# Layer 0's input held as 128 + 64 channels: the group norm, the channel norm and two projections in a new layout

## The chip, the cores and the metric

The kernel runs on one core of one Trainium2 chip. The metric is the device time of one execution in microseconds (us), the smaller the better. The profile is one execution recorded by the hardware profiler; its engines are PE (TensorE matrix multiplies), PEld (the loading of their weights), DVE (VectorE), ACT (ScalarE), POOL (GpSimd) and SP (SyncE, which issues DMAs). Everything is float32.

## The reference, cut to what matters

The input `x` is 16 images of 192 channels by 32 x 32 pixels (1024 pixels each). Four layers follow one another; each adds its result to `x`. Only layer 0 is touched here:

```python
def _gn(v, G=32, eps=1e-5):            # group norm: 32 groups of 6 channels
    g = v.reshape(B_, G, C_ // G, H_, W_)
    m = mean(g, axis=(2, 3, 4)); s = var(g, axis=(2, 3, 4))
    return ((g - m) / sqrt(s + eps)).reshape(v.shape)

# layer 0, on xg = _gn(x); seq is xg as (image, pixel, channel)
h = layernorm(seq) * ln_w + ln_b       # over the 192 channels of a pixel
x_in, z = split(h @ w_up + b_up)       # 192 -> 2 x 384
x_act = silu(causal_conv4(x_in) + conv_b)
q, k, v = x_act @ w_q, x_act @ w_k, x_in
hs = mlstm_scan(q, k, v, gates(q, k, v))          # 12 heads of 32, over 1024 pixels
x1 = seq + ((norm(hs) * mh_w + mh_b + skip * x_act) * silu(z)) @ w_down + b_down
x2 = silu(seq @ w_lin + b_lin)
y = conv3x3(x1 + x2, conv2_w) + conv2_b           # then batch norm over all images
```

Layers 1 to 3 follow for all images (a convolutional attention, a selective scan in four directions, a shift mixer), and take most of the time.

## The kernel before, in words

`layer0` works on one image at a time. Image 0 is written out; images 1 to 15 are 15 turns of a hardware loop (`tc.For_i`, line 753) whose body is `both()` and `image(b, conv3(b - 1))`. Between two turns all engines wait for one another. Within a turn the 3 x 3 convolution of the image before (`conv3`, line 393, tiles `pc`, `ypad`, `w_c`, `w_c2p`) is mixed into this image's work: a part by the tile scheduler, a part at fixed places by `fill(n)` in a stretch with a hand-made order (`tc.manual_schedule`). Outside that stretch the scheduler sets the order of each engine's instructions; each engine then runs its list strictly in that order, and waits where an input is missing.

The 192 channels of `x` lie as two blocks of 96 on 96 partitions (`P6`), each with all 1024 pixels. An image starts like this:

- `group_norm`: four `bn_stats` of 512 pixels (line 90), two `bn_aggr` (line 91), and one matmul with `blk6` (96 x 96, 1/6 inside a group) that gives the means of the groups (line 93, result 96 x 2). Four small DVE steps later a second matmul with `blk6` gives the variances (line 101); then square root on ACT (line 103), reciprocal, and two DVE instructions that write the normalised `xn` (line 109).
- `xnext`, the buffer of the input, is filled for the next image as soon as `xn` is written (line 408, one DMA on SP's queue).
- `channel_norm`: per half of the pixels two matmuls with a 96 x 96 matrix of 1/192 (`on`, line 39 is the helper `matmuls`) give the mean over channels in all rows; DVE subtracts it (line 124), ACT squares (line 126), two matmuls per half sum the squares, ACT takes logarithm and exponential for 1/sqrt (lines 130, 131), and DVE multiplies (line 133), which gives `h`.
- The up projection: for six groups `m` of 128 outputs and two halves, two matmuls of contraction 96 (line 39, `ps<-h,w_up`). For `m` < 3 DVE adds the bias and writes `x_in` (line 427), on which DVE does the causal convolution (lines 437, 441) and ACT the silu (line 445); for `m` >= 3 ACT writes `sz` (line 432).
- Gates: 24 matmuls on column tiles of 32 (line 457) into one PSUM tile, which ACT copies as `raw` (line 464); `spread` matmuls (line 468), scans on DVE, and meanwhile the q and k projections.

In the hand-ordered stretch follow the scores and the chunks of the recurrence (lines 586 to 689). At the end of the image `w_lin` (contraction 96 x 2, on `xn`) and `w_down` (128 x 3) are multiplied for 128 channels of either half and for the last 64 channels of both halves side by side (line 733), and ACT and DVE combine them with the input into `ypad` (lines 737 to 741). For that last step the input is wanted in the layout of the output, and four DMAs on SP's queue make a copy `xr` of `xn` in it (lines 718 to 722).

A matmul of float32 runs on the chip as two passes, each with its own loading of weights; the profile counts each pass.

Of the kernel before, what the change touches and what calls it, by code (L numbers as in the profile page):

```python
# [11 lines left out]
F32 = mybir.dt.float32  # L12
BF16 = mybir.dt.bfloat16
AF = mybir.ActivationFunctionType
ALU = mybir.AluOpType
# [4 lines left out]
C, H, W = 192, 32, 32  # L20
L = H * W
HL = L // 2
P6 = 96
INNER, NH, DH = 384, 12, 32
# [7 lines left out]
def half(hf):  # L32
    return slice(hf * HL, (hf + 1) * HL)


def matmuls(nc, out, pairs):
    n = len(pairs)
    for i, (l, r) in enumerate(pairs):
        nc.tensor.matmul(out, lhsT=l, rhs=r, start=(i == 0), stop=(i == n - 1))


class Ctx:


    def __init__(self, tc, cpool, I):
        self.tc, self.nc, self.I = tc, tc.nc, I
        self.ordered = False
        self.table = None
        nc = self.nc
        self.ident = cpool.tile([128, 128], F32, name="ident")  # L50
        nc.sync.dma_start(self.ident, I["c_ident"])
        self.blk6 = cpool.tile([P6, P6], F32, name="blk6")
        nc.sync.dma_start(self.blk6, I["c_blk6"])
        self.eps5 = cpool.tile([128, 1], F32, name="eps5")
        nc.vector.memset(self.eps5, 1e-5)
        self.one = cpool.tile([128, 1], F32, name="one")
        nc.vector.memset(self.one, 1.0)
        self.on192 = cpool.tile([P6, P6], F32, name="on192")
# [21 lines left out]
        return self.ident[0:k, j : j + 1].to_broadcast([k, m])  # L80


def group_norm(cx, pool, ps, src, dsts):

    nc = cx.nc
    st = pool.tile([P6, 2, 2, 6], F32, tag="gn_st", name="gn_st")
    mv = pool.tile([P6, 2, 2], F32, tag="gn_mv", name="gn_mv")
    for a in range(2):
        for hf in range(2):
            nc.vector.bn_stats(st[:, a, hf, :], src[:, a, half(hf)])  # L90
        nc.vector.bn_aggr(mv[:, a, :], st[:, a].rearrange("p h s -> p (h s)"))
    p = ps()
    nc.tensor.matmul(p[0:P6, 0:2], lhsT=cx.blk6, rhs=mv[:, :, 0], start=True, stop=True)
    mg = pool.tile([P6, 2], F32, tag="gn_mg", name="gn_mg")
    nc.vector.tensor_copy(mg, p[0:P6, 0:2])
    d = pool.tile([P6, 2], F32, tag="gn_d", name="gn_d")
    nc.vector.tensor_sub(d, mv[:, :, 0], mg)
    nc.vector.tensor_mul(d, d, d)
    nc.vector.tensor_add(d, d, mv[:, :, 1])
    p2 = ps()  # L100
    nc.tensor.matmul(p2[0:P6, 0:2], lhsT=cx.blk6, rhs=d, start=True, stop=True)
    rs = pool.tile([P6, 2], F32, tag="gn_rs", name="gn_rs")
    nc.scalar.activation(rs, p2[0:P6, 0:2], AF.Sqrt, bias=cx.eps5[0:P6])
    nc.vector.reciprocal(rs, rs)
    for a in range(2):
        s = src[:, a, :]
        if len(dsts[a].shape) == 3:
            s = s.rearrange("p (h w) -> p h w", w=W)
        nc.vector.tensor_scalar(
            dsts[a], s, mg[:, a : a + 1], rs[:, a : a + 1], op0=ALU.subtract, op1=ALU.mult  # L110
        )


def channel_norm(cx, ps, ones, src, dst, sq, rstd):

    nc = cx.nc
    cx.ln_exp()
    np_ = src.shape[0]
    n = src.shape[1]
    for hf in range(2):  # L120
        pm = ps()
        matmuls(nc, pm[0:np_, :], [(ones, src[:, g, half(hf)]) for g in range(n)])
        for g in range(n):
            nc.vector.tensor_sub(dst[:, g, half(hf)], src[:, g, half(hf)], pm[0:np_, :])
    for g in range(n):
        nc.scalar.activation(sq[:, g, :], dst[:, g, :], AF.Square)
    for hf in range(2):
        pv = ps()
        matmuls(nc, pv[0:np_, :], [(ones, sq[:, g, half(hf)]) for g in range(n)])
        nc.scalar.activation(rstd[:, half(hf)], pv[0:np_, :], AF.Ln, bias=cx.eps5[0:np_])  # L130
    nc.scalar.activation(rstd, rstd, AF.Exp, scale=-0.5)
    for g in range(n):
        nc.vector.tensor_mul(dst[:, g, :], dst[:, g, :], rstd)


def depthwise3(nc, out, pad, w):
# [18 lines left out]
def layer0(tc, cx, NB, ydram, sdram, w1d):  # L155
    nc, I = cx.nc, cx.I
    with ExitStack() as ctx:
# [18 lines left out]
            eng.dma_start(t, v.rearrange("(a p) -> p a", p=p))  # L176
            return t

        xnext = wp.tile([P6, 2, L], F32, name="xnext")
        nc.sync.dma_start(xnext, I["x"][0].rearrange("(a p) l -> p a l", p=P6))  # L180
        w_up = wp.tile([P6, 2, 2 * INNER], F32, name="w_up")
        nc.scalar.dma_start(w_up, I["w_up"].rearrange("(a p) o -> p a o", p=P6))
        ln_w, ln_b = vec("ln_w", P6), vec("ln_b", P6)
        b_up = vec("b_up", 128)

        pre = ctx.enter_context(ExitStack())
# [118 lines left out]
        for m in range(6):  # L305
            matmuls(
                nc, p[:, m : m + 1],
                [(w_up[:, a, m * 128 : (m + 1) * 128], ln_b[:, a : a + 1]) for a in range(2)],
            )
        nc.vector.tensor_add(b_up, b_up, p[:, 0:6])  # L310
        for a in range(2):
# [17 lines left out]


        w_down = wp.tile([128, 3, C], F32, name="w_down")
        w_lin = wp.tile([P6, 2, C], F32, name="w_lin")
        for t, nm, p in ((w_down, "w_down", 128), (w_lin, "w_lin", P6)):
            nc.sync.dma_start(t, I[nm].rearrange("(k p) o -> p k o", p=p))
        w_c2 = wp.tile([128, 9, C], F32, name="w_c2")
        nc.sync.dma_start(w_c2, I["conv2_wT"][0:128])
        w_c2p = wp.tile([128, 2, 3, C], F32, name="w_c2p")
# [65 lines left out]
                nc.scalar.dma_start(stats(slice(128, C))[:, 6 * hf : 6 * hf + 6], st[r, 2, :])  # L403

        def image(b, conv):
            xn = big.tile([P6, 2, L], F32, name="xn")
            group_norm(cx, sm, ps, xnext, [xn[:, 0, :], xn[:, 1, :]])
            nc.sync.dma_start(
                xnext,
                I["x"][bass.ds((b + 1) % NB, 1)].rearrange("o (a p) l -> p (o a) l", p=P6),  # L410
            )
            h = big.tile([P6, 2, L], F32, tag="h", name="h")
            sq = big.tile([P6, 2, L], F32, tag="kT", name="sq")
            rstd = big.tile([P6, L], F32, tag="fc", name="rstd")
            channel_norm(cx, ps, cx.on192, xn, h, sq, rstd)


            sz = big.tile([128, 3, L], F32, name="sz")
            for m in range(6):
                for hf in range(2):  # L420
                    p = ps()
                    matmuls(
                        nc, p,
                        [(w_up[:, a, m * 128 : (m + 1) * 128], h[:, a, half(hf)]) for a in range(2)],
                    )
# [288 lines left out]
                pass  # L714


            xr = big.tile([128, 3, HL], F32, tag="qT", name="xr")
            nc.sync.dma_start(xr[0:P6, 0:2, :].rearrange("p h l -> p (h l)"), xn[:, 0, :])
            nc.sync.dma_start(xr[P6:128, 0:2, :].rearrange("p h l -> p (h l)"), xn[0:32, 1, :])
            lower, upper = slice(0, 64), slice(64, 128)  # L720
            for hf, r in enumerate((lower, upper)):
                nc.sync.dma_start(xr[r, 2, :], xn[32:P6, 1, half(hf)])

            for n in range(3):
                e = n // 2
                parts = [(n, slice(0, 128), slice(0, 128))] if n < 2 else [
                    (0, slice(128, C), lower), (1, slice(128, C), upper)
                ]
                pl, pd = ps(), ps()
                for p, w_, v, k in ((pl, w_lin, xn, 2), (pd, w_down, hT, 3)):  # L730
                    for i in range(k):
                        for hf, o, r in parts:
                            nc.tensor.matmul(
                                p[r, :], lhsT=w_[:, i, o], rhs=v[:, i, half(hf)], start=(i == 0), stop=(i == k - 1)
                            )
                lin = wk2.tile([128, HL], F32, tag="lin", name="lin")
                nc.scalar.activation(lin, pl, AF.Silu, bias=b_lin[:, e : e + 1])
                nc.vector.tensor_add(lin, lin, xr[:, n, :])
                for hf, o, r in parts:
                    x = 0 if r == upper else 1  # L740
                    nc.vector.scalar_tensor_tensor(
# [1351 lines left out]
def constants():  # L2093
# [7 lines left out]
    helmert[DH - 1] = 0.0  # L2101
    return {
        "c_ident": np.eye(128, dtype=f),
        "c_blk6": ((q[:, None] // 6 == q[None, :] // 6) / 6.0).astype(f),
        "c_causal": np.where(p[:, None] <= p[None, :], 0.0, NEG).astype(f),
        "c_hmask": (p[:, None] // DH == np.arange(4 * HW1)[None, :] // HW1).astype(f),
# [66 lines left out]
```

## Time and profile before

| | |
|---|---|
| median of 3 runs | 14432.32 us (14414.68 to 14432.79) |
| the profiled execution | 14423.57 us, span of its instructions 14421.8 us |
| layer 0, from the span's start | about 3055 us of it |
| starts of the turns for images 7, 8 and 9 (first `bn_stats`, line 90) | 1346.74, 1534.80 and 1725.62 us |
| `raw` copy (line 464) of images 7 and 8 | 1391.71 and 1581.19 us |
| busy share of the span | PE 84%, DVE 82%, POOL 76%, ACT 60% |
| mean granted TensorE clock | 0.924 |

Views of the profile used below: stretches of time with each engine's busy time and the granted TensorE clock (PEclk, 1.00 is full speed); the timeline, with runs of the same instruction merged (start in us, us that they span, engine, line, operation, out<-in, rows*columns of the array, out shape, number, and in brackets idle time of the engine ahead of it with what ended it); and the answers for one line of the source (duration of one in ns: least, median, most; then first and last start in us). The ends of matmuls are modelled and pipelined, so distances between starts tell more than durations.

### The profile page before, as it was taken

To read this page: it belongs to the slowest core of one execution; us is meant where nothing else is said; L and a number is where in the kernel's file an instruction comes from. 1 tells how busy PE (TensorE), PEld (TensorE's weight loads), DVE (VectorE), ACT (ScalarE), POOL (GpSimd) and SP (SyncE) were. 2 spreads that over 40 slices of the span, in tenths; PEclk is the share of its full clock that TensorE was granted. 3 is DMA by queue.
4 is the path that set the end of the run, shared out by engine and by line. 5 is a ranking of instruction groups with operands and counts; after the bars stand their busy time and mean duration, and the time that the engine had idled before them with its cause. 6 is when DMAs were issued, how large, how long until landed. Compare 5 with 4: busy or idle time off the path is not lost. (4 is left out here: it accounts for less than half of the span.)

```text
span 14421.8 us, 185702 instructions
## 1 busy us (share of the span) xinstructions
PE 12156.5 (84%) x68912; PEld 4993.1 (35%) x68912; DVE 11832.7 (82%) x9085; ACT 8688.4 (60%) x12229; POOL 10928.7 (76%) x6319
## 2 busy tenths in 40 slices
PE   8999999987888888888888888788888888888877
PEld 4444444442233333333333333333333333333323
DVE  4444444447899999999999999999999999999996
ACT  3333333336667676767676666676676767676655
POOL 2222222216799999999999999999999999999995
PEclk9999999998999999999999999998999999999888
DMA  1000000014344444444444445444444444444432
GB/s 29 15 16 16 15 16 16 16 40 131 128 157 143 157 154 159 153 143 158 143 158 141 160 145 164 142 159 137 162 134 164 147 157 162 145 152 150 144 122 90
DMA packets 702528, 1707.95 MB, mean 118 GB/s; under 512 B 125456, under 2 KB 260065, under 8 KB 693985
## 3 DMA queue, kind: packets, MB, share of 16 engines
q1 hardware_dynamic: 688928, 1693.28, 36.0%
q8 instruction: 556, 9.11, 0.3%
q10 hardware_dynamic: 12736, 3.04, 0.1%
q14 instruction: 308, 2.52, 0.1%
HBM read 1338.12 MB, written 341.15 MB: 116 GB/s over the span
## 5 line engine op out<-in xcount | busy, mean ns | idle before, releaser
L1994 POOL TENSOR_TENSOR xs<-du,bb 128x1024 f32<-128x1024 f32 x3072 | 7196.6, 2364 | 424.9 <-DVE h L2002 418.5
L2002 DVE TENSOR_TENSOR_SCAN h<-h,xs 128x1024 f32<-128x1024 f32 x2688 | 6150.8, 2288 | 385.5 <-ACT h L1987 296.1
L1987 ACT ACTIVATE h<-dl,A 128x1024 f32<-128x1024 f32 x3072 | 3413.9, 1113 | 2420.4 <-DVE hc L2011 2268.5
L2011 DVE TENSOR_TENSOR hc<-h,cb 128x1024 f32<-128x1024 f32 x2688 | 3290.6, 1224 | 264.9 <-DVE h L2002 4.6
L817 PE MATMUL mm<-pad,dg 128*128 128x512 f32 (+1 forms) x5580 | 2667.4, 616 | 120.3 <-DMA dg<-dvd 39.9
L2044 PE MATMUL acc<-hc,sel 128*32 128x256 f32 x24576 | 2016.5, 415 | 800.5 <-DVE hc L2011 600.5
L629 POOL TENSOR_TENSOR D<-D,mask 128x256 f32<-128x256 f32 x768 | 543.6, 741 | 2101.7 <-DVE D L626 2101.7
L2044 PEld LDWEIGHTS acc<-hc,sel 128*32 128x32 f32 x24576 | 549.6, 112 | 2745.4 <-DVE hc L2011 1397.2
L817 PEld LDWEIGHTS mm<-pad,dg 128*128 128x128 f32 (+1 forms) x5580 | 958.7, 182 | 1494.0 <-issue 1285.7
L2007 POOL TENSOR_TENSOR hc<-hc,cb 128x1024 f32<-128x1024 f32 x384 | 905.7, 2359 | 205.1 <-DVE hc L2002 201.9
L817 PE MATMUL mm<-pa,wgt 128*128 128x512 f32 (+1 forms) x1408 | 781.6, 681 | 208.0 <-ACT pb L817 119.6
L2052 PE MATMUL acc<-ones,zero 128*128 128x512 f32 x1648 | 901.6, 678 | 0.0
L2002 DVE TENSOR_TENSOR_SCAN hc<-h,xs 128x1024 f32<-128x1024 f32 x384 | 875.6, 2280 | 16.7 <-ACT h L1987 12.5
L817 POOL TENSOR_TENSOR dlh<-dlh,e 128x512 f32<-128x512 f32 x384 | 489.4, 1275 | 233.5 <-ACT e L817 230.9
L817 POOL TENSOR_TENSOR c<-cx 96x768 f32<-96x768 f32 (+4 forms) x510 | 650.2, 1298 | 2.5 <-PE mm L817 2.5
L817 PE MATMUL mm<-c,xT 128*96 128x256 f32 x2048 | 575.9, 423 | 69.0 <-ACT c L817 68.2
L2031 PE MATMUL acc<-y,ident 128*128 128x512 f32 x576 | 354.2, 700 | 250.1 <-ACT y L2063 248.8
L817 POOL TENSOR_TENSOR duh<-dlh,xx 128x512 f32<-128x512 f32 x384 | 538.1, 1401 | 30.1
L393 PE MATMUL pc<-ypad,w_c 128*64 128x512 f32 (+1 forms) x1152 | 480.3, 664 | 74.3 <-PEq L753 41.5
L2063 ACT COPY y<-acc 128x512 f32<-128x512 f32 x384 | 411.4, 1071 | 150.7 <-PE acc L2044 149.9
L626 DVE SCALAR_TENSOR_TENSOR D<-D,s 128x256 f32<-128x256 f32 x768 | 271.7, 416 | 255.6 <-ACT D L622 255.6
L2052 PEld LDWEIGHTS acc<-ones,zero 128*128 128x128 f32 x1648 | 329.4, 215 | 431.8 <-issue 429.5
(334 smaller groups left out, 15907.5 us busy)
## 6 DMA issues: line engine op xcount, KB each, us to landing
dl<-dld SPq DMA_DIRECT2D x768, 512.0 KB
du<-dud SPq DMA_DIRECT2D x768, 512.0 KB
bb<-xdr SPq DMA_DIRECT2D x256, 512.0 KB
cb<-xdr SPq DMA_DIRECT2D x256, 512.0 KB
dld<-dlh SPq DMA_DIRECT2D x384, 256.0 KB
dud<-duh SPq DMA_DIRECT2D x384, 256.0 KB
dg<-dqd SPq DMA_DIRECT2D x270, 192.0 KB
dg<-dvd SPq DMA_DIRECT2D x180, 144.0 KB
```

Of the source, the lines that this page charges most:

```text
L393: nc.tensor.matmul(p[r, :], lhsT=w_, rhs=v, start=(n == 0), stop=(n == 14))
L629: nc.gpsimd.tensor_mul(d, d, mask)
L817: return f(out, *args, **kw)
L1987: self.nc.scalar.activation(self.h[u % 2], self.dl[n % 2], AF.Exp, scale=self.A[:, blk, n : n + 1])
L1994: self.nc.gpsimd.tensor_mul(self.xs[u % 3], self.du[n % 2], self.bb[blk])
L2002: self.nc.vector.tensor_tensor_scan(o, h, x, 0.0, op0=ALU.mult, op1=ALU.add)
L2007: self.nc.gpsimd.tensor_mul(h, h, self.cb[u % BLOCKS])
L2011: self.nc.vector.tensor_mul(self.hc[u % 3], self.h[u % 2], self.cb[u % BLOCKS])
L2031: nc.tensor.matmul(acc, lhsT=self.cx.ident, rhs=self.y[:, g, half(pair)], start=True, stop=False)
L2044: nc.tensor.matmul(self.acc[rows4(q), q4(s)], lhsT=self.sel, rhs=part(q), start=False, stop=(s + blk == BLOCKS),)
L2052: self.nc.tensor.matmul(self.acc, lhsT=cx.zero.to_broadcast([128, 128]), rhs=cx.ones.unsqueeze(1).to_broadcast([128, 4, 128]), start=False ...
L2063: self.nc.scalar.copy(y.rearrange("p (s w h) -> p s h w" if k % 2 == 0 else "p (s h w) -> p s w h", s=2, **turn), self.acc.rearrange("p (s ...
```

## The change

The input is held as the output's layout wants it: `xnext`, `xn`, `h`, `sq` and `rstd` become [128, 3, 512]: slots 0 and 1 hold channels 0 to 127 of either half of the pixels, slot 2 holds channels 128 to 191 of the first half on partitions 0 to 63 and of the second half on partitions 64 to 127. Weights with the channels as rows (`w_up`, `w_lin`, `ln_w`, `ln_b`) are loaded with the last 64 rows twice, once for either half of the partitions (`twice`). Where two blocks of 96 rows were contracted, now 128 rows are, and then the two halves' 64 rows one after the other, on the upper and the lower 64 rows of the array. The group sums take a new constant `mix` (2 x 2 blocks of 128 x 128) and eight matmuls with one column in place of two with two. `xr` and its four DMAs go; the input is fetched by three DMAs in place of one.

```diff
-    for a in range(2):
-        for hf in range(2):
-            nc.vector.bn_stats(st[:, a, hf, :], src[:, a, half(hf)])
-        nc.vector.bn_aggr(mv[:, a, :], st[:, a].rearrange("p h s -> p (h s)"))
-    p = ps()
-    nc.tensor.matmul(p[0:P6, 0:2], lhsT=cx.blk6, rhs=mv[:, :, 0], start=True, stop=True)
+    for n in range(3):
+        nc.vector.bn_stats(st[:, n, :], src[:, n, :])
+    nc.vector.bn_aggr(mv[:, 0, :], st[:, 0:2, :].rearrange("p h s -> p (h s)"))
+    nc.vector.bn_aggr(mv[:, 1, :], st[:, 2, :])
+    def groups(v):
+        p = ps()
+        for j in range(2):
+            matmuls(nc, p[:, j : j + 1], [(mix[:, i, j, :], v[:, i : i + 1]) for i in range(2)])
+        return p[:, 0:2]
+    p = groups(mv[:, :, 0])
...
-    p2 = ps()
-    nc.tensor.matmul(p2[0:P6, 0:2], lhsT=cx.blk6, rhs=d, start=True, stop=True)
+    p2 = groups(d)
...
+    def sums(v):                       # channel_norm: for the means and for the squares
+        p = [ps() for _ in range(2)]
+        on = cx.on192.to_broadcast([128, 128])
+        for hf in range(2):
+            nc.tensor.matmul(p[hf], lhsT=on, rhs=v[:, hf, :], start=True, stop=False)
+        for hf, r in enumerate(rows2):
+            nc.tensor.matmul(
+                p[hf], lhsT=cx.on192[r].to_broadcast([64, 128]), rhs=v[r, 2, :], start=False, stop=True
+            )
+        return p
+    p = sums(src)
+    for hf, r in enumerate(rows2):
+        nc.vector.tensor_sub(dst[:, hf, :], src[:, hf, :], p[hf])
+        nc.vector.tensor_sub(dst[r, 2, :], src[r, 2, :], p[hf][r])
+    for n in range(3):
+        nc.scalar.activation(sq[:, n, :], dst[:, n, :], AF.Square)
+    p = sums(sq)
+    for hf, r in enumerate(rows2):
+        nc.scalar.activation(rstd[:, hf, :], p[hf], AF.Ln, bias=cx.eps5)
+        nc.scalar.activation(rstd[r, 2, :], p[hf][r], AF.Ln, bias=cx.eps5[r])
     nc.scalar.activation(rstd, rstd, AF.Exp, scale=-0.5)
+    nc.vector.tensor_mul(dst, dst, rstd)
...
             for m in range(6):
-                for hf in range(2):
-                    p = ps()
-                    matmuls(nc, p,
-                        [(w_up[:, a, m * 128 : (m + 1) * 128], h[:, a, half(hf)]) for a in range(2)])
+                pair, o = [ps() for _ in range(2)], slice(m * 128, (m + 1) * 128)
+                for hf, p in enumerate(pair):
+                    nc.tensor.matmul(p, lhsT=w_up[:, 0, o], rhs=h[:, hf, :], start=True, stop=False)
+                for p, r in zip(pair, (lower, upper)):
+                    nc.tensor.matmul(p, lhsT=w_up[r, 1, o], rhs=h[r, 2, :], start=False, stop=True)
...
-            xr = big.tile([128, 3, HL], F32, tag="qT", name="xr")
-            nc.sync.dma_start(xr[0:P6, 0:2, :].rearrange("p h l -> p (h l)"), xn[:, 0, :])
-            nc.sync.dma_start(xr[P6:128, 0:2, :].rearrange("p h l -> p (h l)"), xn[0:32, 1, :])
...
+            pls = [ps() for _ in range(3)]
+            for i in range(2):
+                for n in range(4):
+                    m, hf = min(n, 2), n % 2
+                    r, o = ((lower, upper)[hf], slice(128, C)) if m == 2 else (slice(0, 128), slice(0, 128))
+                    k = (slice(0, 128), (lower, upper)[hf])[i]
+                    nc.tensor.matmul(
+                        pls[m][r, :], lhsT=w_lin[k, i, o], rhs=xn[k, 2 if i else hf, :], start=(i == 0), stop=(i == 1)
+                    )
...
-                nc.vector.tensor_add(lin, lin, xr[:, n, :])
+                nc.vector.tensor_add(lin, lin, xn[:, n, :])
```

The program that results has these differences in the order of PE's list in a loop turn. Before: two convolution matmuls, the group means (1 matmul), one convolution matmul, the group variances (1), four convolution matmuls, the channel means (4), three convolution matmuls, the sums of squares (4), four convolution matmuls, the up projection (24). After: one convolution matmul, the group means (4), one convolution matmul, the group variances (4), four convolution matmuls, the channel means (2 of 128 rows, then the pair of 64 rows), one convolution matmul, the first square sum, one convolution matmul, the second square sum, the pair, six convolution matmuls, the up projection (six times 2 and a pair). The number of convolution matmuls ahead of the up projection is 14 in both. At the end of the image the `w_lin` matmuls all stand ahead of the `w_down` ones. POOL's list is the same in both, and the lists of all engines behind layer 0 are the same but for two small memsets on DVE.

More of the change, by code (lines that the diff above doesn't have):

```diff
@@ L57, in __init__ @@
         nc.vector.memset(self.one, 1.0)
-        self.on192 = cpool.tile([P6, P6], F32, name="on192")
+        self.on192 = cpool.tile([128, 1], F32, name="on192")
         nc.vector.memset(self.on192, 1.0 / C)
@@ L80, in onehot, with group_norm @@
         return self.ident[0:k, j : j + 1].to_broadcast([k, m])
-def group_norm(cx, pool, ps, src, dsts):
+def group_norm(cx, pool, ps, src, dst, mix):
     nc = cx.nc
-    st = pool.tile([P6, 2, 2, 6], F32, tag="gn_st", name="gn_st")
-    mv = pool.tile([P6, 2, 2], F32, tag="gn_mv", name="gn_mv")
-    for a in range(2):
-        for hf in range(2):
-            nc.vector.bn_stats(st[:, a, hf, :], src[:, a, half(hf)])
-        nc.vector.bn_aggr(mv[:, a, :], st[:, a].rearrange("p h s -> p (h s)"))
-    p = ps()
[L93 to L96, printed above, removed]
+    st = pool.tile([128, 3, 6], F32, tag="gn_st", name="gn_st")
+    mv = pool.tile([128, 2, 2], F32, tag="gn_mv", name="gn_mv")
+    for n in range(3):
[8 more added lines that the diff above has]
+    p = groups(mv[:, :, 0])
+    mg = pool.tile([128, 2], F32, tag="gn_mg", name="gn_mg")
+    nc.vector.tensor_copy(mg, p)
+    d = pool.tile([128, 2], F32, tag="gn_d", name="gn_d")
     nc.vector.tensor_sub(d, mv[:, :, 0], mg)
@@ L99, in group_norm @@
     nc.vector.tensor_add(d, d, mv[:, :, 1])
-    p2 = ps()
-    nc.tensor.matmul(p2[0:P6, 0:2], lhsT=cx.blk6, rhs=d, start=True, stop=True)
-    rs = pool.tile([P6, 2], F32, tag="gn_rs", name="gn_rs")
-    nc.scalar.activation(rs, p2[0:P6, 0:2], AF.Sqrt, bias=cx.eps5[0:P6])
+    p2 = groups(d)
+    rs = pool.tile([128, 2], F32, tag="gn_rs", name="gn_rs")
+    nc.scalar.activation(rs, p2, AF.Sqrt, bias=cx.eps5)
     nc.vector.reciprocal(rs, rs)
[L105 to L108, printed above, removed]
+    for i, n in ((0, slice(0, 2)), (1, slice(2, 3))):
@@ L109, in group_norm, with channel_norm @@
         nc.vector.tensor_scalar(
-            dsts[a], s, mg[:, a : a + 1], rs[:, a : a + 1], op0=ALU.subtract, op1=ALU.mult
+            dst[:, n, :], src[:, n, :], mg[:, i : i + 1], rs[:, i : i + 1], op0=ALU.subtract, op1=ALU.mult
         )
-def channel_norm(cx, ps, ones, src, dst, sq, rstd):
+def channel_norm(cx, ps, src, dst, sq, rstd):
     nc = cx.nc
     cx.ln_exp()
-    np_ = src.shape[0]
-    n = src.shape[1]
-    for hf in range(2):
[L121 to L130, printed above, removed]
+    rows2 = (slice(0, 64), slice(64, 128))
+    def sums(v):
[18 more added lines that the diff above has]
+        nc.scalar.activation(rstd[r, 2, :], p[hf][r], AF.Ln, bias=cx.eps5[r])
@@ L131, in channel_norm @@
     nc.scalar.activation(rstd, rstd, AF.Exp, scale=-0.5)
-    for g in range(n):
-        nc.vector.tensor_mul(dst[:, g, :], dst[:, g, :], rstd)
+    nc.vector.tensor_mul(dst, dst, rstd)
 def depthwise3(nc, out, pad, w):
@@ L177, in vec, with fetch, twice @@
             return t
[L179 to L183, printed above, removed]
+        lower, upper = slice(0, 64), slice(64, 128)
+        xnext = wp.tile([128, 3, HL], F32, name="xnext")
+        def fetch(x):
+            nc.sync.dma_start(xnext[:, 0:2, :].rearrange("p h l -> p (h l)"), x[0:128])
+            for hf, r in enumerate((lower, upper)):
+                nc.sync.dma_start(xnext[r, 2, :], x[128:C, half(hf)])
+        def twice(t, src, eng):
+            eng.dma_start(t[:, 0], src[0:128])
+            for r in (lower, upper):
+                eng.dma_start(t[r, 1], src[128:C])
+            return t
+        fetch(I["x"][0])
+        w_up = twice(wp.tile([128, 2, 2 * INNER], F32, name="w_up"), I["w_up"], nc.scalar)
+        ln_w, ln_b = (
+            twice(wp.tile([128, 2, 1], F32, name="v_" + n), I[n].rearrange("(p o) -> p o", o=1), nc.sync)[:, :, 0]
+            for n in ("ln_w", "ln_b")
+        )
+        mix = wp.tile([128, 2, 2, 128], F32, name="mix")
+        nc.sync.dma_start(mix, I["c_mix6"].rearrange("p (i j q) -> p i j q", i=2, j=2))
         b_up = vec("b_up", 128)
@@ L307, in layer0 @@
                 nc, p[:, m : m + 1],
-                [(w_up[:, a, m * 128 : (m + 1) * 128], ln_b[:, a : a + 1]) for a in range(2)],
+                [(w_up[r, a, m * 128 : (m + 1) * 128], ln_b[r, a : a + 1]) for a, r in enumerate((slice(0, 128), lower))],
             )
@@ L331, in layer0 @@
         w_down = wp.tile([128, 3, C], F32, name="w_down")
-        w_lin = wp.tile([P6, 2, C], F32, name="w_lin")
-        for t, nm, p in ((w_down, "w_down", 128), (w_lin, "w_lin", P6)):
-            nc.sync.dma_start(t, I[nm].rearrange("(k p) o -> p k o", p=p))
+        w_lin = twice(wp.tile([128, 2, C], F32, name="w_lin"), I["w_lin"], nc.sync)
+        nc.sync.dma_start(w_down, I["w_down"].rearrange("(k p) o -> p k o", p=128))
         w_c2 = wp.tile([128, 9, C], F32, name="w_c2")
@@ L405, in image @@
         def image(b, conv):
[L406 to L415, printed above, removed]
+            xn = big.tile([128, 3, HL], F32, name="xn")
+            group_norm(cx, sm, ps, xnext, xn, mix)
+            fetch(I["x"][bass.ds((b + 1) % NB, 1)].rearrange("o c l -> (o c) l"))
+            h = big.tile([128, 3, HL], F32, tag="h", name="h")
+            sq = big.tile([128, 3, HL], F32, tag="kT", name="sq")
+            rstd = big.tile([128, 3, HL], F32, tag="qT", name="rstd")
+            channel_norm(cx, ps, xn, h, sq, rstd)
             sz = big.tile([128, 3, L], F32, name="sz")
             for m in range(6):
-                for hf in range(2):
-                    p = ps()
[L422 to L425, printed above, removed]
+                pair, o = [ps() for _ in range(2)], slice(m * 128, (m + 1) * 128)
[3 more added lines that the diff above has]
+                    nc.tensor.matmul(p, lhsT=w_up[r, 1, o], rhs=h[r, 2, :], start=False, stop=True)
+                for hf, p in enumerate(pair):
                     if m < 3:
@@ L714, in image @@
                 pass
-            xr = big.tile([128, 3, HL], F32, tag="qT", name="xr")
-            nc.sync.dma_start(xr[0:P6, 0:2, :].rearrange("p h l -> p (h l)"), xn[:, 0, :])
-            nc.sync.dma_start(xr[P6:128, 0:2, :].rearrange("p h l -> p (h l)"), xn[0:32, 1, :])
-            lower, upper = slice(0, 64), slice(64, 128)
-            for hf, r in enumerate((lower, upper)):
-                nc.sync.dma_start(xr[r, 2, :], xn[32:P6, 1, half(hf)])
+            pls = [ps() for _ in range(3)]
[6 more added lines that the diff above has]
+                        pls[m][r, :], lhsT=w_lin[k, i, o], rhs=xn[k, 2 if i else hf, :], start=(i == 0), stop=(i == 1)
+                    )
             for n in range(3):
@@ L728, in image @@
                 ]
[L729 to L735, printed above, removed]
+                pl, pd = pls[n], ps()
+                for i in range(3):
+                    for hf, o, r in parts:
+                        nc.tensor.matmul(
+                            pd[r, :], lhsT=w_down[:, i, o], rhs=hT[:, i, half(hf)], start=(i == 0), stop=(i == 2)
+                        )
                 lin = wk2.tile([128, HL], F32, tag="lin", name="lin")
                 nc.scalar.activation(lin, pl, AF.Silu, bias=b_lin[:, e : e + 1])
-                nc.vector.tensor_add(lin, lin, xr[:, n, :])
+                nc.vector.tensor_add(lin, lin, xn[:, n, :])
                 for hf, o, r in parts:
@@ L2103, in constants @@
         "c_ident": np.eye(128, dtype=f),
+        "c_mix6": np.stack(
+            [np.stack([(u[:, None] // 6 == v[None, :] // 6) / w for v in (p, 128 + p % 64)], 1)
+             for u, w in ((p, 6.0), (128 + p % 64, 12.0))], 1
+        ).astype(f).reshape(128, 512),
         "c_blk6": ((q[:, None] // 6 == q[None, :] // 6) / 6.0).astype(f),
```

## The prediction

> **What bounds the kernel now.** I read first the stretches, layer 0 and the rest. Columns: from:to, us, then busy us (instructions) of PE, PEld, DVE, ACT and POOL, the granted clock, DMA share, GB/s.
>
> ```profile
> 0.00:3055.00 3055.00, 2866.73 (x22405) 1461.70 (x22406) 1446.36 (x2710) 1142.16 (x2177) 750.26 (x1018) 0.96 0.07 17
> 3055.00:14421.80 11366.80, 9289.80 (x46508) 3531.45 (x46506) 10386.33 (x6375) 7546.25 (x10052) 10178.42 (x5301) 0.91 0.44 146
> ```
>
> The change touches the first line only, a fifth of the span, and there PE is busy 94% of the time. So a turn of image 8 on PE's timeline, from its start at 1534.80 (all times below with a plus sign count from a turn's start):
>
> ```profile
> 1534.85 3.77 PE L393 MATMUL pc<-ypad,w_c 128*128 128x512 f32 x4 [2.96 <-PEq L753]
> 1538.42 0.37 PE L93 MATMUL ps<-gn_mv,blk 96*96 96x2 f32 x2
> 1538.65 2.05 PE L393 MATMUL pc<-ypad,w_c 128*128 128x512 f32 x2
> 1540.50 0.37 PE L101 MATMUL ps<-gn_d,blk 96*96 96x2 f32 x2
> 1540.73 3.76 PE L393 MATMUL pc<-ypad,w_c 128*128 128x512 f32 x8
> 1544.33 3.60 PE L39 MATMUL ps<-xn,on 96*96 96x512 f32 x8
> 1557.50 20.87 PE L39 MATMUL ps<-h,w_up 96*128 96x512 f32 x48
> ```
>
> From the first convolution pass to the end of the up projection at +43.4 PE runs without a gap, and the norm's chain hides between its passes. The first pass of a convolution matmul takes about twice what a later one does: four passes in 3.6 us at the top, eight in 3.6 us below. So next the granted clock (the last figure but two) at two turns' starts:
>
> ```profile
> 1342.94:1346.35 3.41, 0.90 (x6) 0.02 (x2) 1.50 (x2) 0.00 (x0) 0.00 (x0) 1.00 0.00 0
> 1346.35:1349.76 3.41, 2.96 (x4) 1.36 (x5) 2.75 (x7) 1.28 (x1) 0.00 (x0) 0.50 0.41 64
> 1349.76:1353.18 3.42, 3.42 (x12) 1.51 (x12) 1.96 (x7) 1.54 (x2) 0.00 (x0) 1.00 0.12 18
> 1530.67:1534.08 3.41, 1.22 (x6) 0.14 (x2) 1.61 (x3) 0.00 (x0) 0.00 (x0) 1.00 0.00 0
> 1534.08:1537.50 3.42, 2.65 (x3) 1.17 (x4) 2.68 (x7) 1.28 (x1) 0.00 (x0) 0.50 0.29 47
> 1537.50:1540.91 3.41, 3.41 (x9) 1.64 (x8) 0.70 (x5) 0.00 (x1) 0.00 (x0) 0.50 0.23 34
> 1540.91:1544.32 3.41, 3.41 (x8) 1.47 (x9) 1.69 (x3) 1.54 (x2) 0.00 (x0) 1.00 0.15 19
> ```
>
> The clock changes on a fixed grid of 3.413 us. After the wait between turns it is at half, and a window decides over the next: 2.96 us of wide passes brought it back, 2.65 us did not. Two turns are 1725.62 - 1346.74 = 378.88 us, 111 such windows to the hundredth: the loop is locked to the grid. Last, what narrow matmuls do. In setup 60 passes of 24 or 1 columns run back to back:
>
> ```profile
> L39 PE MATMUL ps<-wg,wT x36: 387/387/406, 15.7 to 23.2; 128*128 128x24 f32 x36
> L39 PE MATMUL ps<-v_ln_b,w_up x24: 352/352/352, 23.4 to 28.3; 96*128 96x1 f32 x24
> 40.20 6.46 PE L39 MATMUL ps<-xn,on 96*96 96x512 f32 x8 [7.29 <-DMA v_b_down<-in_b_down]
> ```
>
> One starts every 0.213 us (4.9 us over 23 steps), and the clock is not back afterwards: at 40.20 eight wide passes need 6.46 us, where they need 3.60 in the loop. Some 13 us of narrow matmuls do not count as work for it.
>
> **The change, part by part.** Terms: a wide pass starts every 0.43 us (20.6 us / 48), at half clock every 0.85; a pass of one column every 0.213 at half clock; a result reaches DVE or ACT 0.63 us after its last wide pass starts. A switch of the rows in use costs 0.09 ahead of the first pass and 0.10 behind it, from the starts around 1555.59 (0.52 and 0.53 where 0.43 is usual). Turn as image 8.
>
> *Group norm.* Three statistics for four: the sums are ready at +2.2 (before +2.8). PE has one convolution matmul ahead (+0.05 to +1.9), then eight passes in place of two, 8 x 0.213 = 1.7, to +3.95; the means are copied at +4.2 (before +4.03), the squares of DVE follow in 0.8. They stand behind a convolution matmul at half clock, +5.85; eight passes more, +7.55; square root at +7.7, before +6.1: **+1.6**.
>
> *The clock.* Up to +7.55 only four wide passes ran, half of each window. Borders lie at +2.70, +6.11, +9.53, +12.94 (image 8). The window to +9.53 is full for 1.9 of 3.41 us, less than the 2.65 that failed, so the clock returns at +12.94, before at +6.11. The eight convolution passes that stand ahead of the channel means: 6.1 at 0.85, 1.9 at 0.43, done at +13.66, before +9.53 (1544.33): **+4.1** in all. Image 7's grid gives 13.82. With a border at +7.5, the best place, it is 12.8; the worst is 14.1.
>
> A rule against this reading: the Trainium skill (TensorE: Matmul & The Clock Gate, Part 1) says that the warm-up is 3.4 us of time and not a number of matmuls, so that what is issued after it runs at full rate. By it the one-column passes would keep the gate open and the convolution passes would end near +10.4. The setup rows decide against it. The same skill (TensorEngine Tiling, Instruction Overhead) gives a one-column matmul some 60 cycles; by that the 16 passes would be some 0.8 us in all, not 3.4.
>
> *Channel norm.* Four passes, a switch, the pair (two row halves side by side, two steps): both halves' means reach DVE at +16.63, where before the halves came at +11.45 and +13.16. Four subtractions of 0.6 (64 rows cost as much as 128) end at +19.1, before +14.4. Squares are 3 x 0.53; PE's list holds two convolution matmuls between, so the last pair starts at +20.8 and ACT has the sums at +21.96. Four logarithms of 0.62, not two: exponential at +24.5 (before +19.9); it takes 1.06 x 1.5 less its fixed part, 1.49; the product, now one instruction of 1536, 1.76. `h` is ready at +27.8, PE's remaining convolution passes end at +27.4. Up projection at +27.9, before +22.7: **+5.2**.
>
> *Up projection.* On PE 6 x (4 + 2) passes in place of 48 save 12 x 0.43 = 5.2, twelve switches give back 2.4. But DVE's convolution runs from 1562.10 to 1577.70 without a gap, 15.6 us after the first `x_in` pair, and that pair comes no earlier (+3.1 into the projection for both halves; before +2.0 and +3.8). So DVE ends it, the last silu follows at once (ACT no longer has `sz` ahead, 0.4), and `raw` comes 22.6 us after the projection's start, before 23.7: **-1.1**.
>
> `raw` then stands at +50.4 (before +46.4); with image 7's grid +50.6 (before +45.0). Mean **+4.8**, between 3.1 and 5.9 over all places of the grid.
>
> *End of the image.* `w_lin` needs ten steps for twelve, less three more switches: **-0.2** behind the last passes. The copy `xr` ran at 1505 to 1508 and DVE read it at 1521: its four DMAs were hidden, and taking them away brings nothing; two more DMAs for `xnext` have 180 us.
>
> *The middle.* From `raw` to the next turn it was 143.1 and 144.4 us. In it the clock falls once more (6.8 and 10.2 us at half, at 1435 and 1623). Turns of other length meet the grid elsewhere; where no window is thin enough this spell is gone, worth half of the 5.15 us that PE worked in image 7's, 2.6. Between -2.6 and +0.7 a turn; I take **-1.0**, for a loop that passes that place now and then.
>
> *Setup and image 0.* Eleven more DMAs on the two queues, issues of 0.3 to 0.6 us, and 0.5 MB more at the 158 GB/s of that stretch; the first `xn` waits for DMAs. 0 to 9 us, I take **5**.
>
> Sum: 15 x (4.8 - 0.2 - 1.0) + 5 = 59 us, on the profiled 14423.57 us: 14483. That execution lies inside the three runs and 9 us under their median; I leave it there.
>
> **Rivals.** About 0.2%, 29 us, is what a measurement of this kernel can tell from no change.
>
> *The clock returns as before* (narrow passes count after all, with the convolution passes done at +10.4). Then the start costs 0.9 + 1.1 (norm) - 1.1 - 0.2, some 0.7 a turn, and with setup 14438: no change. The setup rows speak against it. With the cheap end of all unknowns my own sum comes here too.
>
> *Faster:* PE's passes are what counts. Eighteen steps fewer (4 norm, 12 up, 2 `w_lin`) are 7.7 us a turn, less 18 switches of 0.2: 4.1 x 15 - 5, to 14367. For it: PE's full timeline. Against: DVE's gapless 15.6 us, and the norm, a chain with PE in it at two places. It decides only if DVE has over 1.1 us to spare in the up projection; it has none.
>
> *The pairs do not overlap:* then each takes four steps, 24 + 4 steps in place of 16 a turn: 5 us more, near 14540. Against it: three row groups of line 551 run side by side, twelve passes in 1.99 us.
>
> **How the numbers follow.** Forecast 0.68, clock as before 0.16, faster 0.05, pairs apart 0.05, a clock still longer at half (another window, some 1.7 us a turn, 14510) 0.06. The range takes +1.2 to +5.8 us a turn with setup: 14443 to 14517. Slower by over 0.2%: 0.79; within: 0.16; faster: 0.05.
>
> **What would show it.** Right: in the stretches after a turn's start the clock stays 0.50 for some 13 us; the square root at +7.7; up projection at +27 to +28 and 17.8 us long on PE, with DVE's convolution still 15.6; turns of 192 to 195 us. Wrong: a clock back at +6, or turns under 190.

## The result, and the profile after

Twelve runs of the changed kernel have a median of 14456.76 us (14447.27 to 14469.35), twelve of the kernel before beside them 14426.70 us (14414.68 to 14432.79). The ratio is 1.0023, with an interval of 1.0015 to 1.0030: slower by 30 us, where the forecast was 59 us in a range of 14443 to 14517. The profiled execution of the changed kernel took 14456.66 us.

First the two stretches again (from:to, us, then busy us and instructions of PE, PEld, DVE, ACT, POOL, the granted clock, DMA share, GB/s).

```profile
0.00:3055.00 3055.00, 2822.36 (x22524) 1406.20 (x22526) 1414.56 (x2667) 1154.13 (x2217) 749.56 (x1017) 0.97 0.05 13
3055.00:14454.80 11399.80, 9327.32 (x46582) 3541.07 (x46582) 10395.09 (x6386) 7558.15 (x10060) 10178.60 (x5302) 0.91 0.44 145
```

The border at 3055 us is the one that the prediction used, but layer 0 does not end there: its last convolution pass starts at 3092.2 us before and at 3118.0 us after, 25.8 us later. Up to the border PE is less busy (2822 us for 2867) and its mean clock is higher (0.97 for 0.96), yet layer 0 takes longer. The start of the turn and its middle have to be read apart. This is PE's timeline of image 8, from the turn's start at 1547.15:

```profile
1547.21 2.07 PE L422 MATMUL pc<-ypad,w_c 128*128 128x512 f32 x2 [2.97 <-PEq L780]
1549.20 1.86 PE L39 MATMUL ps<-gn_mv,mix 128*128 128x1 f32 x8
1550.92 2.06 PE L422 MATMUL pc<-ypad,w_c 128*128 128x512 f32 x2
1552.77 1.71 PE L39 MATMUL ps<-gn_d,mix 128*128 128x1 f32 x8
1554.34 6.46 PE L422 MATMUL pc<-ypad,w_c 128*128 128x512 f32 x8
1560.63 1.88 PE L126 MATMUL ps<-xn,on 128*128 128x512 f32 x4
...
1574.92 1.95 PE L448 MATMUL ps<-h,w_up 128*128 128x512 f32 x4 [0.47 <-DVE h L144]
1576.81 1.13 PE L450 MATMUL ps<-h,w_up 64*128 64x512 f32 x4
```

From the first of the eight convolution passes to the channel means it is 6.29 us, where it was 3.60; the channel means start at +13.48 (1560.63), before at +9.53; the up projection at +27.77, now released by DVE's `h`. The four passes of a pair of 64 rows span 1.13 us, the four of 128 rows ahead of them 1.95: the pair runs side by side. The clock in the windows of its grid at this start:

```profile
1542.86:1546.27 3.41, 1.38 (x8) 0.21 (x4) 1.50 (x2) 0.00 (x0) 0.00 (x0) 1.00 0.00 0
1546.27:1549.69 3.42, 2.48 (x5) 1.00 (x5) 2.10 (x6) 1.28 (x1) 0.00 (x0) 0.50 0.23 36
1549.69:1553.10 3.41, 3.41 (x12) 2.33 (x12) 0.64 (x4) 0.00 (x0) 0.00 (x0) 0.50 0.26 40
1553.10:1556.51 3.41, 3.41 (x10) 2.38 (x11) 1.44 (x3) 1.55 (x2) 0.00 (x0) 0.50 0.00 0
1556.51:1559.93 3.42, 3.42 (x5) 1.35 (x5) 0.00 (x0) 0.00 (x0) 0.00 (x0) 0.50 0.85 217
1559.93:1563.34 3.41, 3.41 (x10) 1.06 (x9) 0.00 (x0) 0.00 (x0) 0.00 (x0) 1.00 0.05 13
```

PE's busy column is full in the third and fourth line and the clock stays at half all the same; of these 3.41 us the passes of one column took 1.6 in the one and 1.2 in the other. Only the fifth window, full of wide passes, brings the clock back, at +12.78. In the middle of the image the opposite happens. The first three lines are the kernel before, the other three the kernel after; in each PE waits 2.30 us for DVE's `qs`, as the first line says, and the windows around that wait follow:

```profile
1622.67 1.61 PE L615 MATMUL s<-at,itg 32*128 32x128 f32 x13 [2.30 <-DVE qs L555]
1619.42:1622.83 3.41, 1.11 (x10) 0.28 (x5) 3.30 (x6) 0.00 (x0) 0.00 (x0) 1.00 0.00 0
1622.83:1626.25 3.42, 3.42 (x36) 2.98 (x37) 1.22 (x4) 1.26 (x4) 0.27 (x1) 0.50 0.02 5
```

```profile
1639.45 1.21 PE L641 MATMUL s<-at,itg 32*128 32x128 f32 x13 [2.30 <-DVE qs L581]
1635.05:1638.46 3.41, 2.10 (x14) 0.70 (x12) 2.35 (x5) 0.71 (x1) 0.00 (x0) 1.00 0.02 5
1638.46:1641.87 3.41, 2.30 (x38) 1.99 (x39) 1.92 (x5) 0.80 (x3) 0.00 (x0) 1.00 0.00 0
```

Before, the whole wait lay in one window, which held 1.11 us of work, and the clock fell in the next one. After, a border cuts the same wait in two, both windows hold over 2 us, and it stays up. From `raw` to the next turn it is 140.12 us in place of 143.08 and 144.44. A turn of images 3 to 14 takes 191.15 us on average, 56 windows of 3.4133 us (191.15); before it was 189.44.

### The profile page after: what moved, and what is told of

It is laid out like the page before. It is cut to its first block, busy times and chain, and to the rows that moved or that the text cites. A ratio compares the mean times of both kernels' runs of the same rounds, so it can differ in the third digit from the quotient of the medians.

```text
span 14454.8 us, 186120 instructions
## 1 busy us (share of the span) xinstructions
PE 12149.7 (84%) x69104; PEld 4947.3 (34%) x69104; DVE 11809.7 (82%) x9053; ACT 8712.3 (60%) x12277; POOL 10928.2 (76%) x6319
## 5 line engine op out<-in xcount | busy, mean ns | idle before, releaser
L844 PE MATMUL mm<-xd,dtw 108*128 108x512 f32 x768 | 456.7, 679 | 15.6 <-ACT p L844 13.9
```

The costliest lines, as they stand in the source:

```text
L844: return f(out, *args, **kw)
```

## The experiments

Turns are read from the starts of images 3 and 15 in each profile, divided by 12; the layers behind run nearly the same instructions in all kernels, but the stretch behind the last convolution took 11329 to 11348 us in these profiles, so turns tell more than totals. "S" is from a turn's start to `raw`, "M" from `raw` to the next start (turns of images 3 to 14; a single figure is the mean). A "spell" is a stretch at half clock. The ratio is that of the medians of whole executions.

| kernel | S, us | M, us | turn, us | ratio to before (interval) |
|---|---|---|---|---|
| before | 44.97 / 46.39 | 143.08 / 144.44 | 189.44 | 1 |
| after | 51.03 | 140.12 | 191.15 | 1.0023 (1.0015, 1.0030) |
| after_wide | 47.45 to 47.74 | 140.12 | 187.74 | 0.9987 (0.9978, 0.9997) |
| after_tail | 46.05 to 50.89 | 140.18 to 144.31 | 191.43 | 1.0025 (1.0014, 1.0037) |
| before_tail | 44.61 | 143.13 to 144.68 | 187.98 | 0.9987 (0.9977, 0.9997) |
| before_gn4 | 47.24 / 50.59 | 140.51 | 189.15 | 1.0005 (0.9996, 1.0015) |
| before_mid | 44.55 to 47.14 | 140.51 | 185.61 | 0.9962 (0.9946, 0.9977) |
| before_full | 44.61 | 140.58 / 142.18 | 185.86 | 0.9956 (0.9943, 0.9970) |
| after_full | 46.10 | 140.17 (once 141.76) | 186.40 | 0.9973 (0.9962, 0.9983) |
| after_xr | 51.05 | 140.10 | 191.16 | 1.0020 (1.0010, 1.0030) |
| after_apart | 50.94 | 140.46 (once 142.07) | 191.53 | 1.0042 (1.0030, 1.0054) |

**after_wide: the same passes, with 128 columns in place of one.**

```diff
-            matmuls(nc, p[:, j : j + 1], [(mix[:, i, j, :], v[:, i : i + 1]) for i in range(2)])
-        return p[:, 0:2]
+            matmuls(
+                nc, p[:, 128 * j : 128 * j + 128],
+                [(mix[:, i, j, :], v[:, i : i + 1].to_broadcast([128, 128])) for i in range(2)]
+            )
+        return p[:, 0:256:128]
```

> The changed kernel, but the 16 passes of the group sums stream 128 equal columns in place of one; number, order and weights of the passes stay. Theory (the clock's return is what costs, and only streamed columns count for it): a pass of 128 columns costs the same 0.213 us at half clock, but now fills its window, so that the clock returns some 6 us after a turn's start in place of 12.8; the channel means start at +10.1 in place of +13.5, raw at +47.7 in place of +51.05, turns of 187.7 to 188.5 in place of 191.15, about 50 us less in all, near 14405. Rival (it is the number of the passes and the chain through them that cost): no change, turns of 191.1 to 191.2. Third: a pass of 128 columns takes clearly more than 0.213, turns of 191 or more with the clock back early.

The windows of image 8, whose turn starts at 1519.98:

```profile
1519.20:1522.61 3.41, 2.57 (x5) 1.10 (x5) 2.10 (x6) 1.28 (x1) 0.00 (x0) 0.50 0.26 41
1522.61:1526.03 3.42, 3.42 (x12) 2.34 (x12) 0.64 (x4) 0.00 (x0) 0.00 (x0) 0.50 0.23 36
1526.03:1529.44 3.41, 3.41 (x14) 1.97 (x14) 1.43 (x3) 1.54 (x2) 0.00 (x0) 1.00 0.14 16
```

The second line has the same busy time and the same twelve passes as the third line of after above; there the clock stayed at half, here it returns at once, +6.05 in place of +12.78. Raw comes 3.4 us sooner and the turn is 187.74 us, 55 windows to the hundredth (187.73). The number of passes did not change, so what they stream decides: the theory's figures hold, the rival's (191.1) do not. The Trainium skill (TensorE: Matmul & The Clock Gate, Part 1) calls the warm-up a matter of time and not of the number of matmuls; the two kernels agree that the number does not matter, but issuing for 3.4 us is not enough, since twelve passes that fill PE's busy column for 3.41 us bring the clock back in one kernel and not in the other.

**after_tail and before_tail: PE's wait between two turns filled.** Two matmuls that nobody reads stand at the end of each image, behind the last `w_down` (shown for the changed kernel; the kernel before has the same lines).

```diff
+            for i in range(2):
+                tc.keep_in_program_order(nc.tensor.matmul(pls[0][:, 0:448], lhsT=w_down[:, i, 0:128], rhs=hT[:, i, 0:448], start=True, stop=True))
```

> The changed kernel, with two more matmuls of 448 columns (four passes, 1.5 us) at the end of each image, behind the last w_down matmul, where PE waits some 3.5 us for the next turn; nobody reads their result. Theory (the clock): the window in which PE waited is no longer thin, the clock never falls at the turn's start, the square root comes at +5.1 in place of +7.36, the channel means at +8.5 in place of +13.5, raw at +46.0, turns of 186.2 (189.5 at most, where the spell at half clock in the middle comes back): 25 to 75 us less. Rival (not the clock): no change, 191.15, or slightly more from PE's later end.

> The kernel before, with the same two matmuls at the end of each image. Theory (the clock): the start of each turn runs at full clock, raw at +44.35 in each turn in place of +44.97 and +46.39; with 140.3 to 144.4 us behind raw, turns of 184.7 to 188, I take 186 for 189.44: 50 us less in all. Rival (the start is not bound by the clock in the kernel before): no change, 189.4. The difference of this kernel to the changed kernel with the same matmuls is what the change costs without the clock: by my sum +1.7 us up to raw.

In the kernel before it works at the start of the turn as expected: S is 44.61 in every turn (expected 44.35), the start never falls to half, and M keeps its spell. That spell leaves the turn at 187.98, at the top of the range of 184.7 to 188 that was expected (186 was taken), and the whole is 17 us less than before, not 50. In the changed kernel the forecast failed. PE's timeline and the first window of image 8 (start 1546.90):

```profile
1546.96 1.12 PE L422 MATMUL pc<-ypad,w_c 128*128 128x512 f32 x2 [1.34 <-PEq L782]
1549.04 1.07 PE L39 MATMUL ps<-gn_mv,mix 128*128 128x1 f32 x8 [0.95 <-DVE gn_mv L91]
1549.97 2.06 PE L422 MATMUL pc<-ypad,w_c 128*128 128x512 f32 x2
```

```profile
1546.46:1549.87 3.41, 1.96 (x10) 1.16 (x10) 2.10 (x6) 1.28 (x1) 0.00 (x0) 1.00 0.37 58
1549.87:1553.29 3.42, 3.42 (x12) 2.34 (x11) 0.64 (x4) 0.00 (x0) 0.00 (x0) 0.50 0.12 19
```

The turn now begins at full clock (two passes in 1.12 us, not 2.07), but with only one convolution matmul ahead of the group sums PE is done after 1 us and waits 0.95 us; the window holds 1.0 us of wide work and the clock falls inside the turn, for 6.8 to 10.2 us. In images 7 and 9 the border lies elsewhere, the clock does not fall at the start, and S is 46.05, the 46.0 that was expected; M has its spell there (142.75). What I had left out was that a faster start also thins the next window. The kernel before has two convolution matmuls there, and the same filling holds in it; after_full below puts two more matmuls at this place, and its start holds too.

**before_gn4: only the sixteen passes, in the kernel before.**

```diff
-    nc.tensor.matmul(p[0:P6, 0:2], lhsT=cx.blk6, rhs=mv[:, :, 0], start=True, stop=True)
+    def groups(v):
+        p = ps()
+        for j in range(2):
+            matmuls(nc, p[0:P6, j : j + 1], [(cx.blk6, v[:, j : j + 1]), (cx.blk6, cx.zero[0:P6])])
+        return p
+    p = groups(mv[:, :, 0])
...
+    p2 = groups(d)
```

> The kernel before, but each of the two group sums is made of four matmuls of one column (two of them with a zero column) in place of one of two columns: 16 passes for 4, as in the change, and nothing else of it. Theory (the sixteen passes push the clock's return out): the clock returns at about +12.8, square root at +9, channel means at +14.3 in place of +8.1 and +9.5, raw at about +51, no spell at half clock in the middle, turns of 56 windows, 191.15 us: 26 us more, 14453. Rival (the channel norm and the pairs cost it): turns stay at 189.4, raw later by at most 2 us at every second turn.

Half right. In six of the turns of images 2 to 14 the clock returns at +12.6 to +12.8, S is 50.6 to 50.8 and the turn 191.1 to 191.35: the sixteen passes alone do what was seen in the change. In the other seven it returns at +5.9, two windows earlier, S is 47.24 and the turn 187.75. The scheduler put a convolution matmul between the passes of the first sum, so the window that decides (from +2.4 to +5.9) holds 2.86 us of wide passes in nearly all of these turns, between the 2.96 that brought the clock back in the kernel before and the 2.65 that did not. There it goes either way: its border lies within 0.04 us of the same place in most of both kinds of turn. For the whole kernel that leaves 6 us where 26 were expected, not clear of no change. M is 140.51 in all of them, without the spell; the rival (189.4, raw later by at most 2 us) shows in none.

**before_mid: the wait in the middle filled.**

```diff
+            idle = psn.tile([128, HL], F32, name="nd")
+            for i in range(2):
+                tc.keep_in_program_order(nc.tensor.matmul(idle, lhsT=cx.ident, rhs=kT[:, i, 0:HL], start=True, stop=True))
```

> The kernel before, with two more matmuls of 512 columns (four passes, 1.7 us, read by nobody) in the middle of each image, where PE waits 2.3 us for the products qs (line 555). Theory (the second part of the result is the spell at half clock there, which a whole wait inside one window of the clock's grid brings on): no spell at half clock between raw and the next turn, from raw to the next turn 140.5 us in place of 143.1 and 144.4; the start of the turn is as before and moves to where the grid lets it, so turns of 187.7 (55 windows) in place of 189.4: 26 us less. Against it the changed kernel is slower by 191.15 - 187.7 = 3.4 us a turn. Rival (the shorter stretch behind raw comes from the change itself, the missing xr copy or the new order at the end): no change, 189.4.

```profile
1594.82 1.99 PE L551 MATMUL ps<-isc,sel 32*128 32x512 f32 x12
1596.74 1.98 PE L558 MATMUL nd<-kT,ident 128*128 128x512 f32 x4
1599.11 1.21 PE L618 MATMUL s<-at,itg 32*128 32x128 f32 x13 [0.39 <-DVE qs L555]
```

The four passes stand in the wait, of which 0.39 us is left, and nothing behind it moves. M is 140.51 in every turn, to the hundredth what was expected, and the whole difference of 2.6 to 3.9 us is the spell. Before_gn4 has the same 140.51 without any filling. The turn is shorter than I expected: 185.6, not 187.7. I had taken the half clock at the start for given; with turns of another length the border also comes where the start stays at full clock (S 44.55), and the 55 windows do not hold the loop.

**before_full and after_full: the clock held up all turn long.** The kernel before has the two fillings above. The changed kernel has the 128 columns, the filling at the end, two matmuls ahead of the group sums and one in the middle:

```diff
+        if v is not d:
+            for i in range(2):
+                nc.tensor.matmul(p, lhsT=mix[:, 0, i, :], rhs=src[:, i, :], start=True, stop=True)
         for j in range(2):
```

> The kernel before with both fillings, two matmuls at the end of each image and two in the middle. Theory: clock full all turn long, raw at +44.6, then 140.5: turns of 185.1 to 185.3 whatever the grid, 62 to 65 us less than before, 14364. Rival (the fillings get in the way of the work, or the grid holds the turn at 187.7): 187.7, 14402.

> The changed kernel with 128 equal columns in the group sums, two matmuls more at the end of each image, two ahead of the group sums (where PE had only 1 us of wide work and then waited, which brought the clock down again with the matmuls at the end alone) and one in the middle, where the scheduler now also puts a convolution matmul. Theory: clock full all turn long, square root at +5.2, raw at +46.05, then 140.2: turns of 186.2 to 186.4 whatever the grid, 45 to 48 us less than the kernel before, near 14380; 1.0 to 1.2 us a turn slower than the kernel before with its fillings, which is the price of the change itself without the clock. Rival (the change's own price is larger, and was hidden by half clock): turns of 188 or more.

A turn without a spell takes 185.19 and 186.27 us, inside both windows of the forecast (185.1 to 185.3 and 186.2 to 186.4): the change costs 1.08 us a turn when the clock plays no part. The fillings of the two differ, but a stretch at full clock without its own filling is within 0.1 us of the same (M 140.51 and 140.12, S 44.55 in before_mid and 46.05 in after_tail), so they move this price by no more than that. Some turns of before_full have a new spell of one window at +134, worth 1.6 us, so its mean is 185.86. Both are faster than the two kernels of this case, by 64 and 40 us against the kernel before beside them; the unchanged layout with fillings is the fastest.

**after_xr: the copy put back.** Four DMAs of `xn` into `xr`, which the last step reads.

> The changed kernel with the copy xr and its four DMAs put back, and read by the last step as before. Theory: the copy is hidden, turns stay at 191.15, the stretch from raw to the next turn at 140.12. Rival (the copy cost part of what the stretch behind raw lost): that stretch is longer by 0.2 us or more, and turns with it.

Turns of 191.16, M 140.10: the copy is hidden, as the prediction had it.

**after_apart: the pairs taken apart**, on after_full, so that the clock's grid does not blur it.

```diff
-                for hf, p in enumerate(pair):
-                    nc.tensor.matmul(p, lhsT=w_up[:, 0, o], rhs=h[:, hf, :], start=True, stop=False)
-                for p, r in zip(pair, (lower, upper)):
-                    nc.tensor.matmul(p, lhsT=w_up[r, 1, o], rhs=h[r, 2, :], start=False, stop=True)
+                for hf, (p, r) in enumerate(zip(pair, (lower, upper))):
+                    nc.tensor.matmul(p, lhsT=w_up[:, 0, o], rhs=h[:, hf, :], start=True, stop=False)
+                    nc.tensor.matmul(p, lhsT=w_up[r, 1, o], rhs=h[r, 2, :], start=False, stop=True)
```

> The filled changed kernel (clock full all turn long), with the up projection's matmuls half by half: 128 rows, 64 rows, 128 rows, 64 rows, so that no two of 64 rows stand beside each other. Theory (the pairs run side by side, and with them the up projection ends with DVE, without them with PE): every two passes take about 1.05 us, the switches included, so PE ends 25 us after the start of the up projection in place of 17.8, raw 27.5 to 28.5 us after it in place of 23.3, turns of 190.5 to 191.5 in place of 186.27. Rival (DVE ends it in any case): raw moves by under 1 us.

Raw comes 28.12 us after the up projection's start (50.94 - 22.82) in place of 23.29, S grows by 4.84 us and a turn without a spell by 5.1 (191.40 for 186.27). This price holds the twelve additional switches of rows as well as the lost overlap. The pairs are needed: in this layout PE would end the projection without them. With them DVE does, and what they save on PE beyond that is idle.

## Why the prediction was right, and where its sizes were off

The stretches that run at full clock let the 1.71 us a turn be taken apart: S of after_full and before_full, M of after, before_mid and before_gn4. Own price of the change up to `raw`: 46.10 - 44.61 = +1.49. Behind `raw`, without a spell: 140.12 - 140.51 = -0.39. Half clock at the start: (51.03 - 46.10) - (45.68 - 44.61) = 4.93 - 1.07 = +3.86. Half clock in the middle, gone: 140.51 - 143.76 = -3.25. Sum +1.71, and 191.15 - 189.44 = 1.71; the sum closes by its make, so the evidence is in the single terms.

Of the -0.39 only -0.15 lies at the end of the image. The other -0.24 stands right behind `raw`: its first `spread` matmul starts 0.64 us after it, before 0.88, since there PE was still in two convolution passes when `raw` came. From there to the end of the recurrence all steps of the two kernels keep this distance.

| step | predicted | measured (image 8) |
|---|---|---|
| group norm, square root | +7.7 (+1.6) | +7.36 (+1.25) |
| clock back | +12.94 | +12.78 |
| channel means start | +13.66 (+4.1) | +13.48 (+3.95) |
| up projection starts | +27.9 (+5.2) | +27.77 (+5.07) |
| up projection to `raw` | 22.6 (-1.1) | 23.29 (-0.40) |
| S, mean | +4.8 | +5.35 |
| right behind `raw` | none | -0.24 |
| end of the image | -0.2 | -0.15 |
| middle | -1.0 | -3.25 |
| setup and image 0 | +5 | -0.4 (turn of image 1 starts at 206.95, before 207.32) |
| sum | +59 | 15 x 1.71 - 0.4 = +25 in layer 0 (25.8 by its last convolution pass); +30 by the medians |

**The mechanism** held where most of the sum lies: narrow passes do not bring the clock back (after_wide), it returned within 0.2 us of the time given, and DVE's convolution bounds the up projection, 15.7 us without a gap (1579.42 to 1595.14; 15.6 given), while PE is through with it after 17.8 us, as given. Turns of 192 to 195 us were to show it and 191.15 came, for the reason that follows. One reading behind it was weaker than it looked: the eight slow wide passes at 40.20 in setup follow a wait of PE of 7.29 us, and a wait of 2.30 us lowered the clock elsewhere, so they do not prove that the narrow passes left it at half. The trace has no clock record before 45.87 us, but the pace shows it: the 60 narrow passes start every 0.213 to 0.215 us from the second to the last, with no change in 12.6 us, while eight passes of one column at full clock start within 0.93 us (after_tail, 1549.04 to 1549.97), 0.12 each.

**The middle** was the term that was mis-sized, by 2.25 us a turn or 34 us. Two things failed in that step. I bounded the spell by image 7's work alone, 2.6 us, while image 8's costs 144.44 - 140.51 = 3.9, so the mean at stake was 3.25, outside the bound of -2.6. And I took a part of it, "for a loop that passes that place now and then". I had read that the loop before was locked to the grid, and did not carry it over: the loop after is locked too, at 56 windows, so `raw` meets the grid at the same place in each turn and the spell is gone in all of them. Image 1, which starts at another place of the grid, shows the other case in the same run: a spell of 6.8 us and an M of 142.76.

The direction and the loss at the start were reasoned and came as reasoned. Where `raw` would meet the grid was not worked out, so which of the two cases came is chance as far as the prediction goes. With a spell like those before (2.6 to 3.9 us) the turn would have been some 194 to 195 us and the whole near 14496 to 14515 (an estimate: 15 such turns more); without it the total is half of the sum. The range held both.

**The up projection to `raw`** missed by 0.7 us because I had ACT free behind the last silu. Its list still has one `sz` (0.67 us) there and then a table load (1.28 us), and `raw` waits for both: 1596.23, 1596.91, 1598.21 in the trace. The table load stood there before too (1579.89), so the `sz` is the miss.

**Setup** was put at 5 us for eleven more DMAs. The first `bn_stats` in fact started 4.8 us earlier (7.04 for 11.86) and the square root of image 0 4.8 us later (38.19 for 33.42). Neither counted: before, DVE waited 5.41 us more behind that root, for a DMA by the profile (`w1d`), and wrote `xn` from 39.29; after, it wrote `xn` at once, from 38.68. So the DMAs that were to delay the first `xn` did not, and image 1 starts 0.4 us earlier.

**The rivals.** That the clock would come back as before was the case nearest in total (14438) and wrong in kind: the start lost 3.86 us to the clock, and a gain that this rival did not have gave most of it back. "Faster, since PE's passes count" is refuted by the full-clock pair: with the clock out of play the change still costs 1.08 us a turn, the norms +1.88 (up projection at 22.81 for 20.93), the projection -0.40, behind `raw` -0.41 (140.17 for 140.58). "Pairs that do not overlap" is refuted by the trace and priced by after_apart, 4.84 us up to `raw`; the prediction's own 5 us a turn would have made 14558, not the 14540 that it gave.

## What to carry to other kernels

Where a loop's turns wait for each other, look at the granted clock at each turn's start before counting passes: a few narrow matmuls or one wait there can set when the clock comes back, and until then the same wide pass starts every 0.85 us instead of every 0.43. A loop may be held at a whole number of clock windows, so a small saving can vanish and a spell elsewhere can appear or go; price an edit with the clock held up (idle waits of PE filled with wide matmuls that nobody reads) and then separately with the grid. Such fillings were worth 64 us here, more than twice what the change lost.

## What the runs showed of the hardware

- Eight passes of 128 equal columns start within 1.87 us at half clock (1522.02 to 1523.89 in after_wide), eight of one column within 1.72 (1549.20 to 1550.92): nearly the same time, yet only the former brought the clock back.
- A wait of 2.30 us was enough to lower the clock for 6.8 to 10.2 us when it lay inside one window, and did nothing when a border cut it. The Trainium skill (TensorE: Matmul & The Clock Gate, HAM oscillation) gives as the rule that PE should not idle for more than some 3.4 us; here less did.
- Passes on half of the rows may count for less. In image 0 of after_apart the clock stayed at half for 51 us (54.7 to 105.9) under a PE that was busy without a gap from 55.7 on, till 103.8 with two passes of 128 rows and two of 64 rows in turn. Once the clock was up the same mix kept it up:

```profile
62.03:82.51 20.48, 20.48 (x21) 5.14 (x21) 10.12 (x12) 1.15 (x1) 0.00 (x0) 0.50 0.00 0
257.00:277.00 20.00, 20.00 (x39) 5.62 (x38) 16.29 (x18) 3.21 (x4) 0.00 (x0) 1.00 0.00 1
```

That cost image 0 26.6 us (225.86 for 199.24 to the next turn). Whether rows, the switches between them or both make the difference was not tried apart. The switches alone come close: two passes start every 2.00 us here where they would at 0.85 each, so a window holds some 2.9 us of streaming (an estimate from these starts), next to the 2.86 at which before_gn4 went either way.
